# A 3x3 convolution by 4x4 output tiles for four images at once, with its input form stored per image, and two taps per instruction in an attention's logits

## Chip, cores and metric

One Trainium2 chip, one core. The metric is device time in microseconds of one execution (median of the runs). Engines: TensorE (PE in the profile), VectorE (DVE), ScalarE (ACT), GpSimd (POOL), SyncE (SP).

## The reference, cut to what matters

```python
# x: 16 images of 1024 x 32 x 32, all float32
def layer0(x):                                  # a bottleneck with local self-attention
    h = relu(bn(conv1x1(x, w_conv1)))           # 1024 -> 256
    q, k, v = ...                               # three conv1x1 256 -> 256, each with bn (q, k with relu)
    # 32 heads of 8 channels; 9 taps of a 3x3 neighbourhood of k and v
    a = softmax(q . (unfold3x3(k) + pos), over the 9 taps)
    h = relu(bn(sum over taps of a * unfold3x3(v)))
    return relu(bn(conv1x1(h, w_conv3)) + x)    # 256 -> 1024
def layer1(x):                                  # an ordinary bottleneck
    h = relu(bn(conv(x, w1)))                   # 1x1, 1024 -> 256
    h = relu(bn(conv(h, w2)))                   # 3x3, 256 -> 256, padding 1
    return relu(bn(conv(h, w3)) + x)            # 1x1, 256 -> 1024
```

## The kernel before

The 3x3 convolution is done in the transformed domain: VectorE forms sums of neighbouring rows and columns of the input (the input form), TensorE multiplies each of the forms with formed weights, and VectorE adds the products to the outputs (the output form). A tile is 4 rows by 2 columns of outputs, so 6 x 4 = 24 products for 8 outputs, and two images are done together. The stages on TensorE have letters: P = C, Q, V (first convolution, then q, k and v of an image), F (last convolution of layer 0 and first of layer 1), W (3x3), U (last convolution of layer 1, in eight chunks). Their order is a text in the kernel; its end is

```python
        "F12 P15 F13 U11:45 W12 U11:67 U12 U13:0123",
        "F14 F15 U13:45 W14 U13:67 U14 U15",
```

The input form works on whole rows, and its step along columns reads every second element (8 bytes). TensorE's moving operand is dense:

```python
    s = room()                                             # whole rows of 34
    scaled_sum(s, d[2], -4.0, d[4])                        # d[i]: every fourth row, neighbouring columns
    ...
    nc.vector.tensor_tensor(
        v[:, j].rearrange("p n (r w) -> p n r w", w=TC),
        t[:, :, :, j0 : j0 + 2 * TC - 1 : 2],              # step of two elements
        t[:, :, :, j1 : j1 + 2 * TC - 1 : 2], op)
    ...                                                    # cut
    nc.tensor.matmul(acc[i][:, at, n, :], pieces[key][:, m, column % 2, n * P : (n + 1) * P],
        vs[i][:, j, 2 * m : 2 * m + 2, :].rearrange("p b t -> p (b t)"), ...)   # 256 neighbouring elements
```

The logits of the attention take one tap at a time, and the maximum over the nine taps is a tree:

```python
        for k in range(KK):
            nc.vector.tensor_tensor(by_row(t), by_row(qc), kc[:, :, i : i + JROWS, j : j + W], ALU.mult)
            nc.vector.tensor_add(t[:, 0:4], t[:, 0:4], t[:, 4:8])
            nc.vector.tensor_add(t[:, 0:2], t[:, 0:2], t[:, 2:4])
            nc.vector.tensor_add(e[:, k, :], t[:, 0], t[:, 1])
        ...
        tree(ALU.max, mx)                                  # four instructions
```

## Time and profile before

| | before |
|---|---|
| time, median of 2 runs | 2527.45 us (2523.07 to 2531.82) |
| span of the profiled run | 2520.6 us |
| TensorE busy / span less busy | 2470.8 / 49.8 us |
| VectorE busy | 1955.5 us |
| mean granted clock of TensorE | 0.998 |

"Span less busy" is the time in which TensorE has no matmul. As TensorE is the bound, every change of the time must show in one of these two numbers: its work, or its waiting. The page, the groups and the chain of before are in the prediction below; what TensorE waited for stands here (view of waits: engine, line, what it waited for; us in total, times, the longest):

```profile
PE ps L356 <- DMA x<-in_x_dram: 9.5, 1, 9.5
PE ps L437 <- ACT h L956: 6.1, 14, 0.4
```

Apart from the first load, no single wait is over 7 us.

### The profile page before, as it was taken

What the parts mean: (1) busy time and instruction counts of PE and PEld (TensorE: products, weight loads), DVE (VectorE), ACT (ScalarE), POOL (GpSimd) and SP (SyncE); (2) the same over time, 40 slices, a digit from 0 to 9 for tenths busy, and PEclk for the clock granted to TensorE, in tenths of its full rate; (3) what the DMA queues carried; (4) which work ended last, traced back from release to release, by engine and by line L of the source; (5) the groups of instructions that cost most, each with busy time, mean ns of one, the idle gap of its engine ahead of it and who ended that gap; (6) DMA issues with size and microseconds to landing.
All of it is one profiled execution on the core that took longest, in us unless ns stands there. A gap on an engine that the chain in (4) does not pass through costs nothing.

```text
span 2520.6 us, 18901 instructions
## 1 busy us (share of the span) xinstructions
PE 2470.8 (98%) x6536; PEld 1224.1 (49%) x6536; DVE 1955.5 (78%) x1791; ACT 924.5 (37%) x891; POOL 239.5 (10%) x451
## 2 busy tenths in 40 slices
PE   7999999999999999999999999999999999899999
PEld 3443444644455444554445544455445544464464
DVE  6897999899989898989979991899814980993070
ACT  1224133552335524254232542325432533345335
POOL 1020110011000110001110011100100010001000
PEclk9999999999999999999999999999999999999999
DMA  8977677696776977678686777767767768658546
GB/s 304 352 252 258 232 266 238 208 371 235 265 246 228 344 243 259 219 256 327 230 276 228 274 258 252 253 220 273 278 211 236 255 233 269 218 200 303 189 150 234
DMA packets 244719, 638.87 MB, mean 253 GB/s; under 512 B 18576, under 2 KB 125328, under 8 KB 236432
## 3 DMA queue, kind: packets, MB, share of 16 engines
q0 software_dynamic: 63360, 266.89, 30.7%
q1 hardware_dynamic: 141152, 227.83, 28.4%
q10 hardware_dynamic: 40112, 142.94, 14.0%
q8 instruction: 53, 0.87, 0.1%
q14 instruction: 42, 0.34, 0.0%
HBM read 408.47 MB, written 229.11 MB: 253 GB/s over the span
## 4 chain that ended last, share of the span: by engine, by line
PE 84%; DVE 10%; DMA 3%; ACT 2%; issue 1%; ACTq 0%; SPq 0%; DVEq 0%; POOLq 0%
PE ps L387 31%; PE ps L356 30%; PE ps L738 12%; PE ps L437 10%; DVE prod L545 2%; DMA bnk<-kp 2%; DVE acc L609 1%; DVE term L597 1%; PE ps L480 1%; DVE v L665 1%; DVE prod L549 1%; DMA bnk<-bnk 1%; ACT h L956 1%; DVE tv L659 1%; DVE prod L550 1%
## 5 line engine op out<-in xcount | busy, mean ns | idle before, releaser
L356 PE MATMUL ps<-s,u 128*128 128x512 f32 x1024 | 458.4, 592 | 4.3 <-ACT s L400 4.3
L387 PE MATMUL ps<-a,w 128*128 128x512 f32 x1024 | 457.7, 592 | 0.0
L356 PE MATMUL ps<-x,w 128*128 128x512 f32 x1024 | 444.5, 595 | 9.5 <-DMA x<-in_x_dram 9.5
L387 PE MATMUL ps<-y,u 128*128 128x512 f32 x1024 | 441.6, 592 | 3.1 <-ACT ps L380 3.1
L545 DVE TENSOR_TENSOR prod<-qc,bnk 128x2048 f32<-128x2048 f32 x144 | 328.9, 2284 | 137.3 <-DMA bnk<-bnk 136.7
L738 PE MATMUL ps<-v,U 128*128 128x256 f32 x1536 | 338.1, 382 | 18.3 <-issue 7.3
L738 PEld LDWEIGHTS ps<-v,U 128*128 128x128 f32 x1536 | 292.4, 191 | 66.6 <-issue 13.1
L356 PEld LDWEIGHTS ps<-x,w 128*128 128x128 f32 x1024 | 195.4, 191 | 255.3 <-issue 244.9
L356 PEld LDWEIGHTS ps<-s,u 128*128 128x128 f32 x1024 | 194.3, 190 | 250.3 <-issue 235.1
L387 PEld LDWEIGHTS ps<-y,u 128*128 128x128 f32 x1024 | 194.4, 190 | 247.8 <-issue 222.4
L387 PEld LDWEIGHTS ps<-a,w 128*128 128x128 f32 x1024 | 194.6, 190 | 244.9 <-issue 226.0
L400 ACT ACTIVATE s<-ps,par 128x1024 f32<-128x1024 f32 x128 | 142.4, 1112 | 449.8 <-PE ps L387 449.8
L609 DVE TENSOR_TENSOR acc<-acc,term 128x2048 f32<-128x2048 f32 x128 | 293.3, 2292 | 4.4
L597 DVE TENSOR_TENSOR term<-e,bnv 128x2048 f32<-128x2048 f32 x128 | 292.2, 2283 | 0.0
L437 PE MATMUL ps<-h,wqk 128*128 128x512 f32 x512 | 230.4, 598 | 6.1 <-ACT h L956 6.1
L549 DVE TENSOR_TENSOR prod<-prod 128x1024 f32<-128x1024 f32 x144 | 176.3, 1224 | 4.9
L659 DVE SCALAR_TENSOR_TENSOR tv<-vh 128x1224 f32<-128x1224 f32 x32 | 45.0, 1426 | 167.8 <-ACT vh L990 167.8
L400 ACT ACTIVATE r<-ps,bn_sh 128x1024 f32<-128x1024 f32 x128 | 141.9, 1109 | 80.1 <-PE ps L387 79.4
L956 ACT ACTIVATE h<-ps,par 128x1024 f32<-128x1024 f32 x32 | 38.5, 1204 | 338.6 <-PE ps L356 338.6
L437 PEld LDWEIGHTS ps<-h,wqk 128*128 128x128 f32 x512 | 94.7, 190 | 138.9 <-issue 114.4
L380 ACT ACTIVATE ps<-s 128x1024 f32<-128x1024 f32 x128 | 131.4, 1027 | 56.4 <-ACT s L400 39.8
L335 POOL DMA_DIRECT2D r<-r x128 | 67.5, 528 | 888.5 <-DMA out_dram<-r 364.4
(93 smaller groups left out, 1725.5 us busy)
## 6 DMA issues: line engine op xcount, KB each, us to landing
s<-in_x_dram POOLq DMA_DIRECT2D x128, 512.0 KB, 5.8
r<-s ACTq DMA_DIRECT2D x128, 512.0 KB, 3.8
r<-r POOLq DMA_DIRECT2D x128, 512.0 KB, 5.0
out_dram<-r ACTq DMA_DIRECT2D x128, 512.0 KB, 6.1
x<-in_x_dram POOLq DMA_DIRECT2D x120, 512.0 KB, 4.3
U<-uw SPq DMA_DIRECT2D x96, 512.0 KB, 3.8
bnk<-kp SPq DMA_DIRECT2D x32, 680.0 KB, 7.2
bnv<-kp SPq DMA_DIRECT2D x32, 680.0 KB, 6.8
```

Of the source, the lines that this page charges most:

```text
L335: (nc.scalar if kind == "x" and b == 0 else nc.gpsimd).dma_start(t, src)
L356: nc.tensor.matmul(ps[n][:, halves(half)], wt[:, c % (NC // 2), n * P : (n + 1) * P], src[:, halves(half)], start=(c == 0), stop=(c == NC ...
L380: nc.scalar.activation(ps, t, AF.Identity)
L387: nc.tensor.matmul(self.ahead[o][:, halves(half)], pieces[key][:, n, o % (NC // 2) * P :][:, :P], self.src[:, n, halves(half)], start=Fals ...
L400: nc.scalar.activation(t, self.ahead.pop(o), RELU, bias=self.shift(o), scale=1.0)
L437: nc.tensor.matmul(ps[:, halves(half)], pieces[key][:, m, at : at + P], h[:, m, halves(half)], start=(m == 0), stop=(m == NW - 1),)
L545: nc.vector.tensor_tensor(by_row(t), by_row(qc), kc[:, :, i : i + JROWS, j : j + W], ALU.mult)
L549: nc.vector.tensor_add(t[:, 0:4], t[:, 0:4], t[:, 4:8])
L597: nc.vector.tensor_tensor(by_row(dst), rows(e[:, k, :]).unsqueeze(1).to_broadcast([P, HEAD_DIM, JROWS, W]), vc[:, :, i : i + JROWS, j : j ...
L609: nc.vector.tensor_add(acc, acc, t)
L659: nc.vector.scalar_tensor_tensor(to, a, by, b, ALU.mult, ALU.add)
L738: nc.tensor.matmul(acc[i][:, at, n, :], pieces[key][:, m, column % 2, n * P : (n + 1) * P], vs[i][:, j, 2 * m : 2 * m + 2, :].rearrange("p ...
```

## The change

Its intent is fewer matmuls. A tile of 4x4 outputs takes 36 products for 16 outputs, 2.25 an output in place of 3. Four images fill the 256 columns of a matmul, since an image has only 64 such tiles. Four images' forms do not fit beside the rest, so each image's form is made when its input is ready, stored to DRAM, and loaded again for the W stage. W stages are for four images, so the order of stages is new. The formed weights (36 in place of 24 a channel pair) are partly made by ScalarE. The logits' adds take two taps in one instruction, their maximum is one reduction, and Exp is put into ScalarE's order later.

The core of the diff (cut; removed parts are those shown above):

```diff
-NI, NU = 6, 4
-TR, TC = H // 4, W // 2
-TILES = TR * TC
+NI = 6
+NK = 4
+TR = H // 4
+TILES = TR * TR
@@ input form, per image
+        cols = [AP(vh.tensor, vh.offset + j, [vh.ap[0], [PW, lines], [4, TR]]) for j in range(NI)]
+        for make, two in pairs:                          # 12 instructions of 544: read step 16 B, write step 272 B
+            at = [COLUMNS.index(j) for j in two]
+            make([t[:, a].rearrange("p c l -> p l c") for a in at], cols)
+        t = t.rearrange("p j c (m r) -> p (j c m) r", m=NW)
+        for make, two in pairs:                          # 12 instructions of 768: read step 16 B
+            v = [zpool.tile([P, HW], F32, tag="z", name="v")[:, : NI * TILES * NW] for _ in two]
+            make([u.rearrange("p (l r) -> p l r", r=TR) for u in v],
+                 [t[:, :, i : i + 4 * TR - 3 : 4] for i in range(NI)])
+            ...                                          # stored to DRAM
@@ products
+            v = loaded.pop(("V", b, (i, two))).rearrange("p (k j c m r) -> p j m k r c", k=NK, j=2, c=TR, m=NW)
+                        nc.tensor.matmul(acc[i][:, at, :, n, :], pieces[key][:, m, at, n * P : (n + 1) * P],
+                            v[:, at, m], ...)            # innermost step 16 elements, 64 B
@@ output form
+            to = z[i].rearrange("p (n c) -> p c n", c=4)  # writes every fourth element, 16 B
@@ logits
+        for k in range(0, KK, 2):
+            u = t[:, :of]                                # of = 2 taps (the last time 1)
+            nc.vector.tensor_add(u[:, :, 0:4], u[:, :, 0:4], u[:, :, 4:8])
+            ...
-        tree(ALU.max, mx)
+        nc.vector.tensor_reduce(mx, e.rearrange("p k n -> p n k"), AX.X, ALU.max)
@@ end of the order of stages
+        "F12 P15 F13 F14 F15 U10:4567 U11:012345 W12 U11:67 U12 U13 U14 U15",
```

## The prediction

> **What bounds the kernel now.** I read the page's busy table first, then the chain that ended last, then the groups by shape.
>
> ```profile
> PE 2470.8 (98%) x6536; PEld 1224.1 (49%) x6536; DVE 1955.5 (78%) x1791; ACT 924.5 (37%) x891; POOL 239.5 (10%) x451
> ...
> PE 84%; DVE 10%; DMA 3%; ACT 2%; issue 1%; ACTq 0%; SPq 0%; DVEq 0%; POOLq 0%
> ...
> L738 PE MATMUL ps<-v,U 128*128 128x256 f32 x1536 | 338.1, 382 | 18.3 <-issue 7.3
> ```
>
> TensorE is busy in all but 50 us, and the last chain is TensorE for 84%: the kernel is bound by the matmuls, and whatever makes TensorE wait is paid in full. The 3x3 convolution is 1536 instructions and 338.1 us. VectorE at 78% is the second load and has only 565 us free.
>
> The chain in order of time gives the length of the stages. Stages below: P (first convolution, q, k, v of an image), F (expansion and reduction of an image), W (3x3), U (last expansion).
>
> ```profile
> 122.45 27.48 PE ps L356 x64
> 151.22 9.71 PE ps L437 x22
> 162.79 10.50 PE ps L437 x24
> 173.29 27.48 PE ps L356 x64
> ...
> 432.02 41.44 PE ps L738 x192
> ```
>
> The first convolutions of two images start 50.8 us apart, so P is 50.8. A chunk of eight 128x512 instructions is 3.43, so F (16 chunks) is 54.9 and U (8) is 27.5. W for two images is 41.44, or 0.216 us an instruction.
>
> The view of line 545 (the logits' products: first and last start) and VectorE's timeline give an image's attention, the table of DMA issues the way to F (median us to landing last):
>
> ```profile
> L545 DVE TENSOR_TENSOR prod<-qc,bnk x144: 2278/2284/2293, 76.7 to 2177.4; 128x2048 f32<-128x2048 f32 x144
> ```
> ```profile
> 172.77 2.29 DVE L611 TENSOR_TENSOR acc<-acc,se 128x2048 f32<-128x2048 f32 x1
> ```
> ```profile
> a<-acc SPq DMA_DIRECT2D x16, 1024.0 KB, 9.2
> a<-a SPq DMA_DIRECT2D x32, 512.0 KB, 7.4
> ```
>
> Image 0's first product starts at 76.7 and its last multiply ends at 175.1: 98 us. Then its result goes through DRAM. In the same timeline the store is issued at 175.1, the load back at 187.2, and the two activations before F run from 191.1: 18.5 us from VectorE's last instruction to F's first matmul.
>
> **What the Trainium skill says.** "VectorE: DVE Perf Modes", section on the TRN2 errata: an fp32 tensor_tensor of N elements takes (N+151)/0.96 ns. The trace agrees: 2291 against 2284 ns for 2048, 1224 for 1024, 691 against 692 for 512. I use it for the new sizes, 544 and 768. "TensorE: Matmul & The Clock Gate", section on the array as 32x32 blocks: ScalarE and VectorE are strict FIFO. My prediction rests on it: an instruction that waits holds all behind it. "SBUF — State Buffer", section on the port swizzle: lines are 16 bytes, and a step to a new line with every access costs a penalty. The old strided reads (step 8 bytes, 687 ns for 512 elements) pay nothing, so this trace does not test steps of 16 bytes and more, which the change brings.
>
> **The change part by part.**
>
> TensorE. A 4x4 tile takes 36 products for 16 outputs, 2.25 an output; the old 4x2 tile took 24 for 8, or 3. The built program has 576 matmuls (1152 instructions) of 256 columns against 768. Saved: 338.1 x 1/4 = 84.5 us, all on the path. TensorE's work becomes 2470.8 - 84.5 = 2386.
>
> VectorE. Input forms: before, 192 of 512 (120.1) and 96 of 1224 (45.0 + 34.2 + 22.9 + 34.3 = 136.4), so 257 us. After, per image 12 of 544 at 0.724 and 12 of 768 at 0.957: 20.2, or 322 for 16. Output transform: before, 157 (L769, L767, L776, L798, L799). After, per W 24 + 18 + 12 + 4 = about 54 us, 218 for four. Logits: the adds of two taps in one instruction, before 176.3 + 99.7 + 61.3 = 337, after 64 x (2.29 + 1.22 + 0.69) + 37 = 306; the maximum as one reduction of 2304 is 2.56 against 2.77 for the tree. Sum: 1955 + 65 + 61 - 31 - 3 = about 2047. VectorE gets busier, by more than the logits give back.
>
> DMA. Forms add 37.7 MB written and 37.7 MB read; 24 loads of U and 8 of u3 go (16.8 MB). In a W, 36 loads of 0.52 MB in 62 us are 304 GB/s, under the 371 that one slice already reaches, and they are prefetched in six and eight buffers. Hidden.
>
> **What is new on the path.** The order listing of the built programs shows four things.
>
> (a) F15's wait, the large one. F14 and F15 follow each other on TensorE. On VectorE the attention of image 15 is cut: logits, then the form of image 14, then the rest of the softmax and all 18 instructions of the weighted sum. The form of 14 needs F14's output. So whatever the speed of the rest, between the end of F14 and the start of F15 lie: two activations 2.4; form 14 about 19 at these durations with the usual 0.06 overlap of neighbours, plus about 5 because its six outputs have three buffers and wait for stores (a guess from landings of 3 to 7 us), 24; softmax tail 1.22 + 0.69 + 0.42 + 0.42 + 1.75 = 4.5; weighted sum 18 x 2.29 = 41.3; the way through DRAM 18.5. Sum 91, in which TensorE has nothing to do. Being counted from F14's end, no slack earlier absorbs it. Before, the order left two W and U stages there.
>
> (b) W itself. With three z buffers, the second copy of row 5 needs the buffer of row 0, whose VectorE steps stand behind row 4's 16.5 us; I get 3.5 us in the last slot. The first output is complete 10 us after the last matmul, one v or half a U is 7 of them: 3 us. Together 6.8 a W, 27 for four.
>
> (c) The start. The weights of the 3x3 are now formed partly on ScalarE, and seven of their twelve tiles stand before the activation of h in its order, through the same pool of five buffers. Before, h began at 37.9. Seven tiles at about 3 us and two sets of row sums at 6 from 26.4 (when the taps arrive) end near 57, with waits for stores of 10 us somewhat later: about 17 us.
>
> (d) Ordinary waits (h, s, ps: 6.1 + 4.3 + 3.1) stay, 13.5.
>
> Sum: 2386 work + 14.5 before the first matmul + 5 after the last + 17 + 27 + 13.5 + 91 = 2554 us of span. The timed median was 7 over the span, some of it spread; I predict **2555 us**: the 84 us gained in W are lost again in one wait of F15 and smaller ones.
>
> **The rivals.**
>
> Rival 1, the gain comes through: waits (a) to (c) are small or overlap. Then 2386 + 33 + 20 = about 2440 to 2460, 3% faster. For it: the author's stage order was surely tuned. Against it: the instruction order. Even with (b), (c) and the buffer waits at zero, (a) keeps 86 us, and the span is 2386 + 20 + 86 = 2492, 1% faster. Over 2% faster is hardly possible.
>
> Rival 2, TensorE reads slower. The moving operand now steps 64 bytes, a new line for each column. If each took twice as long, 1152 x 0.216 = 249 us come on top: 2800. Against it: fp32 instructions already take 0.84 ns a column, which gives a read more time. I give it one in ten.
>
> Rival 3, VectorE's strided steps are slow (16 bytes read, 272 bytes written). At double time a form is 40; VectorE is nearly gapless from image 8 on, so it would add 20 for form 14 and perhaps 50 through the forms before it: 2620 to 2640. One in eight.
>
> Rival 4, the forms' stores stand behind waiting loads in SyncE's queue and hold VectorE or delay weights: some 10 to 30 us.
>
> **Range and chances.** The centre has a floor of 2492 + 7 below it and only additions above. (c) may be 5 to 25, (a) 86 to 105, (b) 15 to 40. Eight in ten: 2510 to 2615. Faster by over 2% (under 2477): 0.03. Slower by over 2% (over 2578) takes rivals 2, 3 or a bad sum: 0.24. Within: 0.73.
>
> **What would show it.** TensorE busy near 2386 and L721 near 254 us: work right. One gap of 85 to 105 us on TensorE late in the span, released by the load of a, with the form of 14 and the weighted sum of 15 inside it: step (a) right. No such gap, with TensorE busy over 97%: wrong, rival 1. L721 at over 0.25 us an instruction: rival 2. Forms over 0.8 and 1.1 us: rival 3. First h near 55 instead of 37.9: (c).

## The result, and the profile after

The changed kernel is correct and takes **2891.27 us** (2889.55 to 2892.98): 14.4% slower, ratio 1.1439 (95% interval 1.1349 to 1.1530). A ratio, here and below, is the mean time of one kernel's fast runs over that of the kernel before in the same rounds, so not quite the ratio of the medians quoted. The prediction said 2555 with 0.24 for slower.

The page of the changed kernel, its busy times and the chain that ended last by engine:

```profile
PE 2667.3 (92%) x6152; PEld 1178.5 (41%) x6152; DVE 2292.4 (79%) x1585; ACT 926.9 (32%) x873; POOL 275.0 (10%) x523
...
DVE 48%; PE 37%; DMA 9%; ACT 3%; issue 3%; SPq 0%; ACTq 0%; DVEq 0%; POOLq 0%
```

TensorE executes 384 matmuls fewer (6152 against 6536) and is busy 196 us **longer**. The last chain, 84% TensorE before, is VectorE for 48%. Two things went wrong at once, work and waiting: 2667 busy where 2386 was predicted (+281), and 2887.8 - 2667.3 = 220.5 idle where 2555 - 2386 = 169 was (+51).

The groups by shape name the first one (line, engine, operation, shapes, count, then busy us and mean ns of one, then idle time before):

```profile
L721 PE MATMUL ps<-V__2_2341,U 128*128 128x256 f32 x16 | 7.1, 607 | 0.0
...
L646 DVE SCALAR_TENSOR_TENSOR v<-form 128x768 f32<-128x768 f32 x64 | 98.5, 1562 | 43.5 <-DMA v<-v 42.9
...
L646 DVE SCALAR_TENSOR_TENSOR form<-vh 128x544 f32<-128x544 f32 x64 | 72.6, 1157 | 69.0 <-ACT vh L995 69.0
...
L646 DVE SCALAR_TENSOR_TENSOR v<-v 128x768 f32<-128x768 f32 x48 | 46.0, 958 | 1.7
...
L553 DVE TENSOR_REDUCE mx<-e 128x256 f32<-128x2304 f32 x16 | 65.9, 4116 | 0.6
```

Sixteen matmuls of the 3x3 take 7.1 us, 0.444 us each, where before's took 0.216 (the mean of 607 ns is from issue to end and overlaps the next one; read the busy time of the group). And there is a comparison within one kernel: the same operation on 768 elements takes 958 ns where both operands are dense (v<-v) and 1562 where it reads with a step of 16 bytes (v<-form). The reduction takes 4116 ns for 2304 elements, read with steps of 1 KB; what a dense one takes, no run shows.

In the chain in order of time (start, us, what), a W stage for four images is

```profile
2635.46 124.17 PE ps L721 x288
```

against 2 x 41.44 us before: 25% fewer instructions, 50% more time.

The waits of TensorE, and the stretch of VectorE's timeline that lies in the longest of them (start, us, line, operation):

```profile
PE ps L375 <- ACT a L618: 103.2, 3, 91.1
PE ps L344 <- ACT s L388: 46.5, 13, 8.3
...
PE ps L424 <- ACT h L961: 19.2, 16, 12.8
```
```profile
2453.99 2.22 DVE L646 SCALAR_TENSOR_TENSOR form<-vh 128x544 f32<-128x544 f32 x2
...
2482.03 1.53 DVE L646 SCALAR_TENSOR_TENSOR v<-form,v 128x768 f32<-128x768 f32 x1
2483.47 1.23 DVE L562 TENSOR_TENSOR tree<-e 128x1024 f32<-128x1024 f32 x1
...
2527.39 2.29 DVE L594 TENSOR_TENSOR acc<-acc,se 128x2048 f32<-128x2048 f32 x1
```

In these lines a is the attention's output as ScalarE hands it to F, s the output of layer 0 as ScalarE hands it to layer 1's first convolution, h the output of layer 0's first convolution; ps is a bank of PSUM, and z, below, ScalarE's copy of the products of W.

The wait of 91.1 us ends at 2538.7, where F15 starts. Inside it lie the form of image 14, the rest of the softmax, the weighted sum of image 15 and its way through DRAM: the prediction's step (a). That it agrees to the microsecond is luck: three of its terms were off and cancelled (see below).

### The profile page after: what moved, and what is told of

Read it like the earlier page. It is cut to its first block, busy times and chain, and to the rows that moved or that the text cites. A ratio compares the mean times of both kernels' runs of the same rounds, so it can differ in the third digit from the quotient of the medians.

```text
span 2887.8 us, 18175 instructions
## 1 busy us (share of the span) xinstructions
PE 2667.3 (92%) x6152; PEld 1178.5 (41%) x6152; DVE 2292.4 (79%) x1585; ACT 926.9 (32%) x873; POOL 275.0 (10%) x523
## 4 chain that ended last, share of the span: by engine, by line
DVE 48%; PE 37%; DMA 9%; ACT 3%; issue 3%; SPq 0%; ACTq 0%; DVEq 0%; POOLq 0%
PE ps L721 16%; PE ps L375 12%; DVE acc L581 9%; DVE acc L592 8%; PE ps L344 7%; DVE prod L533 7%; DVE form L646 5%; DMA v<-v 4%; DVE prod L538 4%; DVE v L646 3%; DVE prod L539 2%; PE ps L424 2%; DMA u<-in_u1t_dram 2%; DVE mx L553 1%; DVE e L540 1%
## 5 line engine op out<-in xcount | busy, mean ns | idle before, releaser
L375 PE MATMUL ps<-a,w 128*128 128x512 f32 x1024 | 465.8, 600 | 112.2 <-ACT a L618 103.2
L344 PE MATMUL ps<-s,u 128*128 128x512 f32 x1024 | 475.7, 610 | 46.7 <-ACT s L388 46.5
L375 PE MATMUL ps<-y,u 128*128 128x512 f32 x1024 | 447.8, 599 | 14.8 <-ACT ps L368 14.5
L581 DVE TENSOR_TENSOR acc<-e,bnv 128x2048 f32<-128x2048 f32 x144 | 327.5, 2284 | 3.7
L592 DVE TENSOR_TENSOR acc<-acc 128x2048 f32<-128x2048 f32 x128 | 293.4, 2292 | 4.4
L538 DVE TENSOR_TENSOR prod<-prod 128x2048 f32<-128x2048 f32 (+1 forms) x80 | 166.2, 2078 | 2.6
L741 ACT ACTIVATE z<-ps 128x1024 f32<-128x1024 f32 x48 | 49.2, 1024 | 370.8 <-PE ps L721 360.9
L368 ACT ACTIVATE ps<-r 128x1024 f32<-128x1024 f32 x128 | 131.2, 1025 | 66.6 <-ACT r L388 40.3
L748 DVE TENSOR_TENSOR z<-z 128x1024 f32<-128x1024 f32 x24 | 29.4, 1225 | 134.6 <-ACT z L741 134.6
L320 POOL DMA_DIRECT2D x<-in_x_dram x120 | 63.5, 529 | 750.6 <-PE ps L344 576.3
```

The source lines that it names most:

```text
L320: (nc.scalar if kind == "x" and b == 0 else nc.gpsimd).dma_start(t, src)
L344: nc.tensor.matmul(ps[n][:, halves(half)], wt[:, c % (NC // 2), n * P : (n + 1) * P], src[:, halves(half)], start=(c == 0), stop=(c == NC ...
L368: nc.scalar.activation(ps, t, AF.Identity)
L375: nc.tensor.matmul(self.ahead[o][:, halves(half)], pieces[key][:, n, o % (NC // 2) * P :][:, :P], self.src[:, n, halves(half)], start=Fals ...
L538: nc.vector.tensor_add(u[:, :, 0:4], u[:, :, 0:4], u[:, :, 4:8])
L581: nc.vector.tensor_tensor(by_row(dst), rows(e[:, k, :]).unsqueeze(1).to_broadcast([P, HEAD_DIM, JROWS, W]), vc[:, :, i : i + JROWS, j : j ...
```

## The experiments

The letters in the expectations: **A**, TensorE is slowed by the step of its moving operand; **C**, VectorE is slowed by the steps of the forms (and of whatever else steps by 16 bytes or more); **D**, the order on VectorE around F15 costs what the prediction's step (a) says; **E**, formed later: once the strides are gone, the end is set by what VectorE does before F15. Each has its rivals in its text. All are variants of the changed kernel. Those that compute a wrong result are named so; the others are correct. Labels stand in brackets, because the expectations refer to one another by them.

### The moving operand read in runs of eight (e1_pe_runs)

```diff
-  .rearrange("p (k j c m r) -> p j m k r c", ...)
+  .rearrange("p (k j c m r) -> p j m k c r", ...)
```

The same 256 elements in another order: runs of eight neighbours (32 bytes) in place of single elements 64 bytes apart. The result is wrong.

> Only the order in which TensorE walks the moving operand of the 3x3 changes: runs of 8 neighbouring elements (32 bytes) instead of single elements 64 bytes apart; the result is wrong on purpose (each tile grid transposed). Theory A (the 64-byte step doubles the matmul): sixteen 128x256 instructions take 3.45 us again instead of 7.1, TensorE's busy time falls from 2667 by about 249 to near 2415, and the time by 160 to 240 (part is lost to VectorE, which was busy for 2292 us), so 2650 to 2730. Rival B (the 4x64 form of the output, the accumulation or the loads of V slow it): sixteen instructions stay at 7.1 us and the time stays within 10 of 2891.

Measured: 2727.59 us, ratio 1.0801 (1.0782 to 1.0820). TensorE's busy time is 2448.9, 218 us less; the time falls by 164, because TensorE's idle time rises from 220.5 to 277.0. The largest new wait is for ScalarE's copies of the products, which the slow matmuls had hidden:

```profile
PE ps L721 <- ACT z L741: 35.2, 8, 7.8
```

Theory A holds. Where a slow stage covers other work, its cost is not all of what its removal gives.

### The same, with the result right (e1_pe_runs_correct)

The copies and sums that take the products out of PSUM read them back in the old order, so that the outputs are correct:

```diff
-  nc.scalar.activation(t, acc[i].rearrange("p a k n t -> p (a k n t)"), ...)
+  nc.scalar.activation(t by (n r c), acc[i].rearrange("p a k n (c r) -> p (a k n) r c", c=TR), ...)
   # and likewise in the two sums with a PSUM bank
```

> The same walk of TensorE with a correct result: ScalarE's copy and VectorE's two reads of the sums put the tiles back in order by stepping 32 bytes in PSUM. Theory A: TensorE as in the run before. If a step of 32 bytes in PSUM costs as steps in SBUF do, the copy of 1024 goes from 1.02 to about 2 us and the two adds (1.13 us already, their output steps 16 bytes) stay or rise; the time is then 0 to 25 us above that run's. If not, both are equal within 10 us.

Measured: 2728.11 us, ratio 1.0788 (1.0756 to 1.0819), the same as the wrong one. In its groups by shape, sixteen matmuls:

```profile
L721 PE MATMUL ps<-V__2_6367,U 128*128 128x256 f32 x16 | 3.6, 379 | 0.0
```

ScalarE's copy takes 1024 ns with the 32-byte step in PSUM as without, so a one-line change of an index order and its counterpart give 164 us back at no cost.

### The forms read and written densely (e2_forms_dense)

```diff
-  cols = [AP(vh.tensor, vh.offset + j, [vh.ap[0], [PW, lines], [4, TR]]) ...]
+  cols = [AP(vh.tensor, vh.offset + j, [vh.ap[0], [PW, lines], [1, TR]]) ...]
   # likewise the write of t, and in the second half [t[:, :, i : i + TR] for i in range(NI)]
```

Its output is wrong, which doesn't matter for the time. The same number of instructions and elements, neighbouring ones.

> Only the forms' access changes: neighbouring elements in place of steps of 16 bytes on reading and 272 bytes on writing; same instructions and sizes, wrong result on purpose. Theory C (steps double VectorE's time per element): the 544s go from 1.16 to 0.72 us and the strided 768s from 1.56 to 0.96, VectorE's busy time from 2292 to about 2130; the forms and the waits that hang on VectorE shorten, time 2891 to 2790-2850, TensorE's 3x3 unchanged at 7.1 us for sixteen. Rival: the pattern's short rows of 8 cost it: durations stay and so does the time.

Measured: 2811.02 us, ratio 1.1141 (1.1111 to 1.1171); VectorE 160 us less busy.

```profile
L646 DVE SCALAR_TENSOR_TENSOR v<-form 128x768 f32<-128x768 f32 x64 | 59.8, 955 | 62.5 <-DMA v<-v 61.8
...
L646 DVE SCALAR_TENSOR_TENSOR form<-vh 128x544 f32<-128x544 f32 x64 | 44.6, 718 | 68.7 <-ACT vh L995 68.7
```

The durations are those that the prediction had assumed, the time is 80 us lower, the wait of F15 falls to 79.3 us and TensorE's waits for s from 46.5 to 17.4. Theory C holds. VectorE is not the busiest engine, and half of what it was relieved of still came through. Only 12 us of that are F15's wait; 29 are TensorE's waits for s, which in the changed kernel are 13 short ones, none over 8.3 us.

### The form of image 14 behind the attention of image 15 (e4_form14_late)

```diff
-  side.first(transform(b), side.tensor + CHUNK + 6.0, ...)
+  at = 1e5 if b == 14 else side.tensor + CHUNK + 6.0
+  side.first(transform(b), at, at if b == 14 else ...)
```

> Only VectorE's order changes: the form of image 14 (29.5 us) stands behind the attention of image 15 instead of in its middle. Theory D (F15's 91 us wait is this order): TensorE's gap before F15 falls from 91 to about 61 us and the time by about 30 to near 2860. Rival (the wait is the way through DRAM or something on ScalarE): gap and time stay within 8 us.

Measured: 2869.27 us, ratio 1.1367 (1.1343 to 1.1392), 22 us less. The waits of TensorE:

```profile
PE ps L375 <- ACT a L618: 76.2, 2, 64.0
```

F15's wait is 27 us shorter, where 30 was expected, and the time 22 where about 30 was. Theory D holds in kind: what VectorE does between F14 and F15 is what F15 waits for. Not all of it comes back as time: in the profiled runs the other waits grow by 9 us (those for h by 4) and TensorE's busy time by 5.

### Both strides removed, with the result right (e5_dense_correct)

The input of the 3x3 is stored sorted by row and column modulo four. Both steps of the form then read neighbouring elements (runs of 8, then of 64), write dense, and the moving operand becomes 64 neighbouring elements an image:

```diff
-  vh = const.tile([P, NW * (H + 2), PW], ...)
+  VL, PHASES = 35, (26, 0, 9, 18, 27, 1)      # where padded column (or row) 4c+j, j = 0..5, begins
+  vh = const.tile([P, NW * VL, VL], ...)
+  # ScalarE writes it, four activations a half: to row 9*(h%4) + h//4, column 9*(w%4) + w//4
-  cols = [AP(vh.tensor, vh.offset + j, [vh.ap[0], [PW, lines], [4, TR]]) for j in range(NI)]
+  cols = [AP(vh.tensor, vh.offset + at, [vh.ap[0], [VL, lines], [1, TR]]) for at in PHASES]
+  ... [t[:, :, at * TR :][:, :, :TILES] for at in PHASES]        # rows: 64 neighbouring elements
-  v = ...rearrange("p (k j c m r) -> p j m k r c", ...)
+  v = ...rearrange("p (k j m t) -> p j m k t", ...)
```

> Correct result. The hidden map of the 3x3 is now stored sorted by its row and column modulo four (35 lines of 35 in place of 34 of 34), so that both steps of the input form read and write neighbouring elements (12 of 560 and 12 of 768 an image) and the moving operand of TensorE is 64 neighbouring elements for each image; ScalarE writes the map in eight activations in place of two. Theory A+C (the two strides are what the prediction missed, and their costs are independent): sixteen undisturbed matmuls of the 3x3 3.5 us (from 7.1), form steps about 0.74 and 0.96 us, TensorE busy near 2450, VectorE near 2135, time 2891 less 163 (moving operand alone) less 80 (forms alone), about 2650; the wait of F15 about 80. Rival (the costs of the changed kernel lie elsewhere as well, in stores, loads or ScalarE): 2700 or more, because the eight strided activations or the transfers hold what VectorE no longer holds. Rival the other way (shorter forms only show their worth once TensorE reads at full speed): 2600 or less.

Measured: 2615.74 us (2611.91 to 2619.59), ratio 1.0352 (1.0331 to 1.0373): 276 us under the changed kernel, 32 more than the two parts alone (164 + 80). So their effects are not independent, in the direction of the second rival but less than it said: with both gone, the waits that the first experiment had are shorter (for the copies 22 us in place of 35, for s 15 in place of 45). Two groups by shape, and a wait of TensorE:

```profile
L722 PE MATMUL ps<-V__2_8229,U 128*128 128x256 f32 x16 | 3.6, 379 | 0.0
...
L647 DVE SCALAR_TENSOR_TENSOR v<-form 128x768 f32<-128x768 f32 x64 | 59.8, 955 | 66.8 <-DMA v<-v 66.2
...
PE ps L722 <- ACT z L742: 22.0, 4, 5.5
```

### The maximum as a tree, and the form of image 14 late (e6_dense_tree_late)

The last kernel plus the edit of image 14, plus

```diff
-  nc.vector.tensor_reduce(mx, e.rearrange("p k n -> p n k"), AX.X, ALU.max)
+  # tree of four tensor_tensor with ALU.max, as in the kernel before
```

> Correct result. As e5_dense_correct, and the maximum of the nine taps as a tree of four instructions again (2.8 us by the trace of the kernel before, in place of 4.1 for the reduction with its steps of 1 KB) and the form of image 14 put behind the attention of image 15. VectorE 22 us less busy than in e5 (16 x 1.35). The wait of F15 about 64 or less (from about 80). Time: if the wait of F15 is the only place where VectorE's order counts, 15 to 22 us under e5, about 2630; if VectorE's load also sets the waits of the later stages, 30 to 45 under e5.

Measured: 2591.81 us, ratio 1.0253 (1.0228 to 1.0278), 24 us less; F15's wait 60.2, VectorE 22 us less busy. It is between the two cases of the expectation, nearer to the first; how the 24 us divide between the two edits was not measured. What VectorE itself waits for now:

```profile
DVE v L662 <- DMA v<-v: 72.4, 16, 34.9
DVE v L651 <- DMA v<-v: 63.4, 16, 8.5
```

These are 136 us (35 of them in one wait late in the span), in the second half of the forms: six outputs of an image share three buffers, an output can only be made when an earlier one is stored, and the median store of an output lands after 5.3 us.

### The costs by themselves: a sweep of steps (e7_step_sweep)

Its output is wrong, which doesn't matter for the time. The four W stages read their operand with steps of 8, 16, 32 and 128 bytes, and the second half of the forms reads with 8, 12, 32 and 64 bytes, four images each.

```diff
+  v = {0: v[:, 0:512:2], 4: v[:, 0:1024:4],
+       8: v.rearrange("p (a b) -> p b a", b=8)[:, 0:2], 12: v.rearrange("p (a b) -> p b a", b=32)[:, 0:8]}
-  v[:, at, m],
+  v[b],
+  step = (2, 3, 8, 16)[b // NK]        # the forms' read step, in elements
```

> Wrong result on purpose: a measurement of the disputed costs by themselves. The four W stages read their moving operand with steps of 8, 16, 32 and 128 bytes (W0, W4, W8, W12), and the second steps of the forms read with steps of 8, 12, 32 and 64 bytes (images 0-3, 4-7, 8-11, 12-15; 768 elements, dense output). Theory A (each read of a new 16-byte line costs TensorE a second slot): 16 matmuls take 3.5 us at 8 bytes and 7.1 at 16, 32 and 128. Rival for A (only steps of 64 bytes and more are slow): 3.5 at 8, 16 and 32 and 7.1 at 128. Theory C (VectorE has one price for any step from 16 bytes on): 0.96 us at 8 and 12 bytes, 1.56 at 32 and 64. Rival for C (the price grows with the step): over 1.7 at 32 and over 2 at 64.

One run, 2859.07 us (its state is unknown; only durations are read from it). Sixteen matmuls of W0, W4, W8 and W12, from the groups by shape:

```profile
L733 PE MATMUL ps<-V__0_2335,U 128*128 128x256 f32 x16 | 3.8, 387 | 0.0
...
L733 PE MATMUL ps<-V__0_4297,U 128*128 128x256 f32 x16 | 7.4, 628 | 0.0
...
L733 PE MATMUL ps<-V__0_6263,U 128*128 128x256 f32 x16 | 7.5, 638 | 0.0
...
L733 PE MATMUL ps<-V__0_7964,U 128*128 128x256 f32 x16 | 7.1, 607 | 0.0
```

And VectorE's 768 elements, the same view cut to the stretch of each four images:

```profile
L646 DVE SCALAR_TENSOR_TENSOR v<-form 128x768 f32<-128x768 f32 x16 | 14.9, 954 | 16.5 <-DMA v<-v 16.5
...
L646 DVE SCALAR_TENSOR_TENSOR v<-form 128x768 f32<-128x768 f32 x16 | 19.0, 1208 | 16.2 <-DMA v<-v 16.2
...
L646 DVE SCALAR_TENSOR_TENSOR v<-form 128x768 f32<-128x768 f32 x16 | 24.5, 1550 | 12.3 <-DMA v<-v 12.1
...
L646 DVE SCALAR_TENSOR_TENSOR v<-form 128x768 f32<-128x768 f32 x16 | 23.5, 1491 | 8.7 <-DMA v<-v 8.5
```

| step of the read | 8 B | 12 B | 16 B | 32 B | 64 B | 128 B |
|---|---|---|---|---|---|---|
| TensorE, sixteen matmuls (dense 3.6 us) | 3.8 | - | 7.4 | 7.5 | 7.1 (changed kernel) | 7.1 |
| VectorE, 768 elements (dense 955 ns) | 954 | 1208 | 1562 (changed kernel) | 1550 | 1491 | - |

The price follows how many elements share a line of 16 bytes. Two (8 bytes) cost VectorE nothing and TensorE next to nothing (3.8 against 3.6); one (16 bytes and more) costs twice on TensorE and 1.6 times on VectorE. At 12 bytes, where lines are shared now and then, VectorE lies between, where the expectation had put it at the dense price. Both rivals, a limit only at 64 bytes or a price that grows with the step, are out.

### Attention between the pairs of a form (e8_forms_interleaved)

After each pair of a form's outputs, VectorE does two pieces of the running attention (some 9 us) while the outputs are stored:

```diff
+  if job.get("rest") and other and at <= self.vector:
+      return other, at            # the attention first, while the form rests
+  job["begun"], job["rest"] = True, 2 if cost == 4.5 else 0
   # cut: each piece of attention that is done takes one from "rest"
```

> Correct result. As e6_dense_tree_late, and between the pairs of a form's six outputs VectorE now does two pieces of the running attention (some 9 us) while the outputs just made are stored, where before it stood and waited for one of the three buffers. Theory E (with the strides gone, VectorE is what F15 waits for, and its 136 us of waits for the forms' stores are the largest thing to be had there): waits of VectorE for the forms' stores 136 down to under 40, the wait of F15 from 60 to 0 to 30, the time 30 to 60 us under e6, 2530 to 2560, so about even with the kernel before. Rival (those waits lie where VectorE would have waited for projections or for ScalarE anyway): the waits only change their name, and the time stays within 10 us of e6.

Measured: **2549.74 us** (2547.87 to 2553.25), ratio 1.0095 (1.0078 to 1.0112): 42 us less. Waits of VectorE, then of TensorE:

```profile
DVE v L662 <- DMA v<-v: 39.8, 4, 35.0
...
DVE v L651 <- DMA v<-v: 17.9, 6, 6.8
```
```profile
PE ps L376 <- ACT a L623: 43.4, 2, 42.4
PE ps L726 <- ACT z L746: 38.1, 7, 9.9
```

The waits for stores are 58 us, not under 40, and F15 waits 42.4, not 0 to 30; the time is in the range expected. Of the 58, 35 are one wait in the form of image 14 while F15 runs. There the prediction's rival 4 shows itself: in SyncE's timeline the stores are issued only at 2291.57, behind two loads of weights issued at 2280.86, while VectorE has stood still since 2261. It costs nothing here, since TensorE has no wait over 2 us between 2257 and 2409. This is the fastest correct version of the changed kernel that ran, and still 1% slower than the kernel before, by an interval that leaves out 1.

### Half of U10 before F15 (e9_interleaved_u10_first)

```diff
-  F13 F14 F15 U10:4567 U11:012345 W12
+  F13 F14 U10:4567 F15 U11:012345 W12
```

> Correct result. As e8, and half of U10 stands between F14 and F15 on TensorE in place of behind F15. Theory E: where F15 still waits for VectorE, four chunks (13.7 us) fill that wait, but they are then missing behind F15, where they cover the form of image 15; so within 8 us of e8, either way. If F15 waits less than 14 us in e8, this is slower than e8 by up to 14.

Measured in the same rounds: 2554.83 us, ratio 1.0117 (1.0102 to 1.0132). F15 waits 28.4 us, 14 less as expected, and the time does not fall: the intervals overlap, and TensorE now waits 10 us once for a weight of W (U). This one change of the order gives nothing; others were not tried.

### One tap per instruction again (e10_one_tap)

```diff
-  for k in range(0, KK, 2): ... u = t[:, :of]
+  for k in range(KK):       ... u = t[:, k % 2 :][:, :1]
```

> Correct result. As e8, but the logits' adds take one tap per instruction again, as before the change: 144 + 144 + 144 instructions of 1024, 512 and 256 in place of 80 each. By the durations of the two kernels' traces (1.224, 0.692, 0.425 us against 2.290, 1.225, 0.692) VectorE gets 144 x 2.341 - 64 x 4.207 - 16 x 2.341 = 30 us more to do, 1.9 an image. Theory E (in e8 the end is set by VectorE's work before F15): the wait of F15 rises by the part that VectorE has no idle time for, at least the 4 us of images 14 and 15 and at most 30, and the time with it: 5 to 30 us slower than e8. Rival (e8 is held by something else, and VectorE has room): within 4 us of e8.

Measured: 2555.74 us, ratio 1.0117 (1.0094 to 1.0139), against 1.0095 (1.0078 to 1.0112): 6 us slower by the medians, with overlapping intervals. VectorE is 26 us busier, and F15's wait rises by 3.2 us, about the 4 us of images 14 and 15. That is theory E at its lowest end, and nearly the rival: of VectorE's total little counts, and the rise fits the reading that only what it does shortly before F15 does. The two taps per instruction, right by themselves, are worth some us at the most here, within the noise.

### Exp put into ScalarE's order at once (e11_exp_at_once)

```diff
-  if job["b"] == 0:
-      self.fire()
+  self.fire()
```

> Correct result. As e8, but the Exp of every image stands in ScalarE's order where VectorE's differences are expected to be ready, not held back until the planned time of TensorE has passed it. Theory E: VectorE's waits for Exp (91 us) shrink by 20 to 50, the last multiply of attention 15 comes earlier, and F15's wait of 42 us shrinks by up to that much; the time falls by 5 to 30 us. Rival: ScalarE then waits for VectorE in its own order (20 us in e8, then more) and hands TensorE its sums late: new waits of TensorE for s, ps or h, and a time equal to e8 or above.

Measured: 2554.31 us (2544.89 to 2559.68), ratio 1.0111 (1.0083 to 1.0138). Inconclusive: the time is the one that the rival gave, but neither side's waits moved. VectorE's waits for Exp are 92.6 us (91.6), F15's wait is 42.1 (42.4), and ScalarE's waits for VectorE before Exp are 20.0 (20.5). The edit moved next to nothing, so it says nothing on what a late Exp is worth.

### The output form written densely (e12_z_dense)

Its output is wrong, which doesn't matter for the time. On the interleaved version:

```diff
-  to = z[i].rearrange("p (n c) -> p c n", c=4)
+  to = z[i].rearrange("p (c n) -> p c n", c=4)
```

> Wrong result on purpose. As e8, but the output form writes its four columns as four dense blocks in place of every fourth element (16-byte step). The last stride of the change that the prediction had priced as free: in e8 72 steps of 512 elements take 1.09 us and 48 sums with a PSUM bank 1.08, where 512 dense elements take 0.69. Theory C (a 16-byte step costs VectorE the same everywhere): 0.69 us each, VectorE 120 x 0.40 = 48 us less busy, and since this work holds ScalarE's copies and with them the products of W, TensorE's waits for z fall from 38 to under 20; with a part of the rest taken from F15's wait of 42: time 20 to 40 us under e8, about 2520, even with the kernel before. Rival (these steps lie beside the products and TensorE waits for something else in W): VectorE falls, the waits for z stay, and the time stays within 8 us of e8.

Measured: **2528.13 us** (2525.32 to 2533.13), ratio 1.0008 (0.9992 to 1.0025): even with the kernel before. From the groups by shape and the waits of TensorE:

```profile
L749 DVE SCALAR_TENSOR_TENSOR z<-z 128x512 f32<-128x512 f32 x72 | 45.5, 686 | 0.8
```
```profile
PE ps L376 <- ACT a L623: 42.7, 2, 41.7
PE ps L726 <- ACT z L746: 26.8, 7, 10.2
```

686 ns against 1092 with the 16-byte write step; VectorE is 42 us less busy. The waits for z fall by 11, less than expected, and F15's wait does not move: as with one tap an instruction, work that lies elsewhere is not what F15 waits for. No correct version of this edit was run: the outputs would have to be interleaved somewhere else.

## Why the prediction was wrong

The account from the changed kernel downwards, in microseconds (the time is the median, the other columns are of the profiled run):

| removed | time | step | TensorE busy | TensorE idle (span less busy) | F15's wait |
|---|---|---|---|---|---|
| (the changed kernel) | 2891.3 | | 2667.3 | 220.5 | 91.1 |
| strides of TensorE's operand and of the input forms | 2615.7 | 276 | 2423.5 | 194.4 | 79.3 |
| reduction's stride; form of 14 before the sum of 15 | 2591.8 | 24 | 2421.2 | 176.7 | 60.2 |
| VectorE standing while forms are stored | 2549.7 | 42 | 2412.8 | 138.7 | 42.4 |
| stride of the output form (wrong) | 2528.1 | 22 | 2410.4 | 121.0 | 41.7 |

The steps depend on their order, and the last is no kernel that could be used. They take off 363 us, nearly 300 of them by removing strides. That the last row lies at the time of the kernel before is a coincidence: it is busy for 60 us less and idle for 71 more.

- **The failed step is TensorE's work, 2386 in the sum and 2667.3 measured: the moving operand's step was priced as free, and rival 2, which said otherwise, was given too little weight** ("Against it: fp32 instructions already take 0.84 ns a column, which gives a read more time. I give it one in ten"). Its size was right: the prediction said 249 us more for TensorE at twice the duration, and the W stage is 124.2 us for four images in place of the 62 assumed, 4 x 62 = 248. Most of the other 33 us are a halved clock (below). The argument against rival 2 rested on no row of the profile: none said how long a read may take. The page of the Trainium skill that the same text cites ("SBUF — State Buffer", the note on cachelines in the section on the DMA port swizzle) gives the rule that applied, at least two hits on a line for full bandwidth, and the sweep agrees with it: 8 bytes 954 ns, 12 bytes 1208, 16 bytes 1562. The prediction had even written down that the old steps of 8 bytes do not test the new ones, and should have left the chance open.
- **Rival 3 came with it.** The two were weighed as separate accidents of 1 in 10 and 1 in 8, but in the sweep both set in at the same step, 16 bytes: here they came true together. Together they add 314 to 334 us to 2555, which gives 2869 to 2889 against the 2891 measured; the closeness is partly luck, since removing both gave only 276. Forms at 1.6 times their price (predicted: 0.724 and 0.957; measured 1.157 and 1.562) cost 80 us alone, close to the 65 to 85 over 2555 that rival 3 gave, but not by its path: it gave 20 of them to F15's wait, which fell by 12. Steps were priced as free in two more places: the output form (0.69 predicted, 1.09 to 1.15 measured, 0.69 once its step was removed) and the reduction (2.56 against 4.12, where the step as the cause was not tested by itself).
- **Step (a), the wait of F15, was right**: 91 predicted, 91.1 measured. But three terms of the sum were off and cancelled, so the agreement is luck: the form of 14 took 29.5 us in place of 24, its start came 6.3 us after F14 in place of 2.4 (softmax steps lie before it), and the way through DRAM took 9.0 in place of 18.5. Image 0's 18.5 us, and the medians of the whole kernel (9.2 and 7.4), were too long for this stretch: here the store took 3.85 and the load 3.85. Taking form 14 out of it shortened the wait by 27.
- **Step (b)**, 27 us in the W stages, could not show while the matmuls were slow. With them at speed the waits for the copies are 22 to 38 us: right in size, and partly due to the output form's stride.
- **Step (c)**, 17 us at the start, 5 to 25 in its range: h starts at 50.2 in place of 37.9, and TensorE waits 12.8 for it. Right.
- Slips in its sums do not matter to the result. The 14.5 us before the first matmul count the 5 after the last twice (the first matmul starts at 9.5), the two parts of (b) are 6.5 and not 6.8, and the parts shown for the output form add to 58 a W where 54 is written (the durations of dense instructions give 54).
- **What was not in the sum at all**: in e5, where the strides of TensorE and of the input forms are gone, TensorE is busy 2423.5 and idle 194.4, together 63 over the prediction's 2386 and 169. Some 30 of the 37 us of work are a halved clock after waits: all stretches but the last in which the trace of e5 grants 0.50 begin 2 to 5 us after the start of a wait of TensorE (not every wait has one). Half of TensorE's busy time in such stretches is, by an estimate from the clock records, 34 us in e5, 34 in the changed kernel and 4 before. In the interleaved version the granted clock is 0.50 from 2257 to 2263, after F15's wait, and 1.00 then; the first sixteen matmuls take 10.1 us, elsewhere 7.0. Part of the idle time hangs on the forms' waits for their stores; the prediction had 5 us for one image ("a guess") and rival 4 had 10 to 30; the interleaving showed 42.
- That the interleaved version lands at 2549.7, beside the 2555 predicted, confirms nothing of the sum: it has no form of 14 before F15 and hides the stores, and still has the output form's stride.
- **What remains open**: why F15 still waits 42 us in the interleaved version can be followed to VectorE's chain from the W before (attention 14 ends at 2133, attention 15 at 2248, and VectorE has no gap over a microsecond between), but no run removed it. One part of that chain might be moved like the form of image 14, which no run tried: the form of image 13 stands inside the attention of image 15, from 2182 to 2213, and takes some 20 us of VectorE there. So whether the larger tile can beat the kernel before is not settled; here the best correct version loses by 1%, with 58 us less work on TensorE and 89 us more waiting.

## What to carry to other kernels

Count products and bytes last, and innermost steps first: a layout that puts the innermost index 16 bytes or more apart turned a 25% saving of matmuls into 50% more time for the stage, and another order of the same indices gave 164 us back. When two rivals share a cause, give them one chance together, and do not argue a cost away with a margin that no row of the profile shows. An engine with 20% of its time free can still set the end: look at what it does between two stages that follow each other directly on the bound engine.

## What the Trainium skill lacked or had wrong

- "SBUF — State Buffer", the note on cachelines in the section on the DMA port swizzle: its rule (two hits on a 16-byte line for full bandwidth) agrees with the sweep, but the figure that follows it, "4 fp32" to stride for free, does not: four fp32 are 16 bytes, one hit on a line, and cost 1562 ns in place of 955 for 768 elements. Free were two fp32 (954 ns); three cost 1208.
- The same place, and "Advanced Engine Details and Errata", section "SBUF Cachelines", name a penalty without its size: it is a factor of 1.6 on VectorE (1562 to 955, 1157 to 718, 1092 to 686), and it does not grow from 16 to 64 bytes, nor when read and write both step (1157 for 544 elements).
- "TensorE: Matmul & The Clock Gate" does not say that the step of the moving operand counts: 0.44 to 0.47 us in place of 0.22 for a 256-column fp32 instruction at 16 to 128 bytes, with steps of 8 bytes (3.8 us for sixteen) and runs of eight elements (3.6) next to free.
- "VectorE: DVE Perf Modes", section on the TRN2 errata, gives the time of an fp32 instruction by its elements alone; it held for dense operands (958 to 957 ns) and is 1.6 times too short for a step of 16 bytes.
- "PSUM — Partial Sum Buffer", specifications, warns that an access pattern that is not contiguous slows matmuls; it does not say how other engines fare. ScalarE's read of 1024 elements with a step of 32 bytes took 1024 ns, as without.
